# A four-layer graph network on one core: where the adjacency is checked for low bits, and where the branch on it stands

## The chip, the core and the metric

The kernel runs on one core of one Trainium2 chip. A core has TensorE (PE, matrix products into PSUM banks), VectorE (DVE), ScalarE (ACT), GpSimd (POOL) and SyncE (SP), which here issues most of the loads; each engine runs its own instructions in the order in which they were written for it, and waits on semaphores for the others. Transfers from main memory are done by DMA engines. The metric is the time of the program on the device, in microseconds (us).

## The reference

There are N = 2708 nodes with 128 features and an adjacency matrix of 2708 x 2708 in fp32. Four layers, each with a layer norm and a rectifier before it and a residual sum after it, use the adjacency:

```python
# layer 0: attention weights, used with adj.T twice
C = alpha_src[None, :] + alpha_dst[:, None]
Tau = adj_matrix.T * jnp.exp(jnp.maximum(0.2 * C, C))
att_weights = Tau / jnp.sum(Tau, axis=1, keepdims=True)
Z = adj_matrix.T * att_weights @ H
# layer 1: relu of (normalised adj + identity) @ x @ weight
# layer 2: adj.T @ x / degree, two linear maps, batch norm, relu
# layer 3
Z1 = leaky_relu(s_row[:, None] + s_col[None, :], negative_slope=0.01)
den = jnp.exp(Z1)
num = jnp.matmul(A, den)
att = jnp.where(num != 0, den / jnp.where(num != 0, num, 1.0), 0.0)
H = jnp.matmul(A, jnp.matmul(att, XW))
```

In the inputs the adjacency holds only zeros and ones.

## The kernel before

The adjacency and its transpose lie in main memory. It is worked through in T = 22 tiles of 128 rows (the last has 20), each 2708 wide; a width is also split in six blocks of up to 512 columns (one PSUM bank each), or in two halves of 1536 and 1172 columns (COLS).

Layer 0 is in lines 274 to 420. A first loop (298 to 313) over the six blocks makes the layer norm, its transposes, the rows `row_a` of exponentials and the projections `hs`. A second loop (347 on) goes over the 22 tiles. For each half of a tile, ScalarE makes `tau` (L355), VectorE finishes it and multiplies it by the adjacency (L358, L361), and TensorE adds up `hs` times the result into six accumulators (`aggregate`, L224) and the column sums (L367). ScalarE also sums the degrees of each tile (`degrees`, L341). The tiles come through a pool `stream` of NSTREAM = 4 buffers, so a load waits until all readers of an older tile are done. For the last two tiles the aggregation is kept back, and the degree is summed on VectorE (L339). The accumulators are then copied to `hT` (`evacuate`, L215 and L217).

Layers 1 to 3 use a cheaper form of fp32 products where a matrix can be taken to be exact in a shorter format. TensorE multiplies tiles of type fp32r ("float32r"): the adjacency is converted to it (by ScalarE and VectorE, `rows`), and the other operand is split in a high and a low part. This is right only if no entry of the adjacency has bits set in the low half of its 32. So `check` (L292 to L294) reads the lower 16 bits of each element of a tile on ScalarE and writes their sum into a column of `low`. It runs once per tile in layer 0: for the first three tiles in the first loop (L310), for the others with the degrees (L345). Its other output, as wide as the tile, is thrown away into a buffer `junk`.

After layer 0 these sums become one number, `flag` (L395 to L402). All engines read it and branch (L1289, L1290):

```python
some_low = nc.values_load(flag[0:1, 0:1], min_val=0, max_val=1, skip_runtime_bounds_check_because="0 or 1")
with tc.If(some_low > 0) as general:
    with ExitStack() as s3:
        rest(False, s3)
with general.Else():
    with ExitStack() as s3:
        rest(True, s3)
```

`rest(exact, stack3)`, from L486, is layers 1 to 3. With these inputs the second side, with exact = True, is executed. Layers 1 and 2 (`product_by_halves`, L248) stream the matrix in halves of tiles, through dflat (three places, filled ahead at L388 during layer 0), row_b and pools; each half is converted (L529) and multiplied (L224). Layer 1 starts with `finish0` (L555), which turns the accumulators of layer 0 back, adds the residual and makes the layer norm, with `dis`, made from the degrees, as a factor.

Layer 3 sorts the nodes, takes sums of rows, and then has 22 steps (L1183 on): products into two PSUM banks in turn (L1206), a logarithm on ScalarE that frees each bank (L1211), a subtraction on VectorE (L1214), an exponential on ScalarE (L1220) and the product into the accumulators (L1150). These are copied out (L1235), turned and split (L1241, L1242). Last comes `product` (L232, called in L1287), over all 22 tiles of the transposed adjacency: `load_rows` (L1271) brings a tile into one of six places in turn, ScalarE (tiles 0 to 3) or VectorE (the others) converts it (L1283), TensorE multiplies it by the two parts. The last four tiles (NLAST) are done block by block, and `finish3` (L1247) copies each block, turns it, adds the residual and stores it.

The order of instructions on an engine comes from a scheduler that may move them by priority, except where `tc.keep_in_program_order` holds them; it does so within one side of a branch and not across it.

Of the kernel before, what the change touches and what calls it, by code (L numbers as in the profile page):

```python
# [8 lines left out]
F32 = mybir.dt.float32  # L9
# [10 lines left out]
def kernel(  # L20
# [19 lines left out]
    nc = tc.nc  # L40
# [46 lines left out]
    const = ctx.enter_context(tc.tile_pool(name="const", bufs=1))  # L87
# [13 lines left out]
    nc.vector.memset(xs[:, TF:, :], 0.0)  # L101
    for t0 in range(0, TF, 4):
        t1 = min(t0 + 4, TF)
        nc.sync.dma_start(
            xs[:, t0:t1, :], x[t0 * P : t1 * P, :].rearrange("(t p) d -> p t d", p=P)
        )
    nc.sync.dma_start(xs[:TAIL, TF, :], x[TF * P :, :])
# [166 lines left out]
    with ExitStack() as stack:  # L274
        stream = stack.enter_context(tc.tile_pool(name="stream", bufs=NSTREAM))
        edge = stack.enter_context(tc.tile_pool(name="edge", bufs=3))

        def load_rows(src, t):
            return fill(stream.tile([P, N], F32, tag="a", name="a"), src, t)

        low = const.tile([P, T], F32, name="low")
        nc.gpsimd.memset(low, 0.0)

        def junk(t):
            return dflat[:, :N] if t < 8 else hT[:, :N]  # L290

        def check(t, a):  # L292
            lower = a.bitcast(U16).rearrange("p (n h) -> p n h", h=2)[:, :, 0]
            return nc.scalar.activation(junk(t), lower, AF.Identity, accum_out=low[:, t : t + 1])  # L294

        first_rows = []
        done = 0
        for b in range(NB):
            layernorm(b, hn)
            p = bank()  # L300
            turned(p, hn, TILES[b])
            nc.vector.tensor_copy(hT[:, spans(b)], p[:, : len(TILES[b]) * P])
            p = acc_bank(b % 2)
            w = len(TILES[b]) * P
            nc.tensor.matmul(p[:, :w], w0_spread[:, 1, :], hT[:, spans(b)], start=True, stop=True)
            tc.keep_in_program_order(nc.scalar.activation(row_a[:, spans(b)], p[:, :w], AF.Exp, scale=-0.8))
            if b < 3:
                first_rows.append(load_rows(adj, b))
            else:
                tc.keep_in_program_order(check(b - 3, first_rows[b - 3]))  # L310
            while done < T and min(done + 3, T) <= TILES[b][-1] + 1:
                project(w0_ext, done, acc_bank(2 + done // 3 % 2))
                done += 3
        e_hi = const.tile([P, T], F32, name="e_hi")
        e_lo = const.tile([P, T], F32, name="e_lo")
        e_neg = const.tile([P, T], F32, name="e_neg")
        nc.scalar.activation(e_hi, hs[:, :, P], AF.Exp)
        nc.scalar.activation(e_lo, hs[:, :, P], AF.Exp, scale=0.2)
        nc.vector.tensor_scalar_mul(e_neg, e_hi, -1.0)
        pick = const.tile([P, NB, NB], F32, name="pick")  # L320
        nc.vector.memset(pick, 0.0)
        for b in range(NB):
            nc.vector.memset(pick[:, b, b : b + 1], 1.0)


        GR = 3
        ones_at = const.tile([P, NB // GR, 32], F32, name="ones_at")
        nc.vector.memset(ones_at, 0.0)
        for i in range(NB // GR):
            nc.vector.memset(ones_at[:, i, i : i + 1], 1.0)  # L330
        deg = const.tile([P, T], F32, name="deg")
        nc.gpsimd.memset(deg, 0.0)
        accs = [acc_bank(b) for b in range(NB)]
        den = bank()
        waiting = []

        def degrees(t, a):
            if t >= T - 2:
                nc.vector.tensor_reduce(deg[:, t : t + 1], a, AX.X, ALU.add)  # L339
            else:  # L340
                m = nc.scalar.activation(junk(t), a, AF.Identity, accum_out=deg[:, t : t + 1])  # L341
                if t < 3:
                    tc.keep_in_program_order(m)
            if t >= 3:
                check(t, a)  # L345

        for t in range(T):
            a = first_rows[t] if t < 3 else load_rows(adj, t)
            late = t >= T - 2
            rhs = (yT, row_b)[t % 2]  # L350
            for h, (h0, h1) in enumerate(COLS):
                w = h1 - h0
                tau = edge.tile([P, w], F32, tag=f"tau{h}", name=f"tau{h}", bufs=3)
                at2 = rhs[:, h0:h1]
                nc.scalar.activation(  # L355
                    tau[:, :w], row_a[:, h0:h1], AF.Relu, bias=e_neg[:, t : t + 1], scale=e_lo[:, t : t + 1]
                )
                nc.vector.scalar_tensor_tensor(  # L358
                    tau[:, :w], tau[:, :w], e_hi[:, t : t + 1], a[:, h0:h1], ALU.add, ALU.mult
                )  # L360
                nc.vector.tensor_mul(at2[:, :w], a[:, h0:h1], tau[:, :w])  # L361
                if not late:
                    aggregate(hs[:, t, :P], rhs, accs, t == 0, False, range(3 * h, 3 * h + 3))
                for b in range(3 * h, 3 * h + 3):
                    lo, hi = E0[b]
                    g = 32 * (b % GR)
                    nc.tensor.matmul(  # L367
                        den[g : g + 32, : hi - lo],
                        ones_at[:, b // GR, :],
                        tau[:, lo - h0 : hi - h0],  # L370
                        start=(t == 0 and b < GR),
                        stop=(t == T - 1 and b >= GR),
                    )
            waiting.append((t, a))
            if t >= 2:
                degrees(*waiting.pop(0))
            if t == 6:
                w1_sb = load("w1_sb", [P, P], w1, nc.sync)
                wn_sb = load("wn_sb", [P, P], w_n, nc.sync)
                wc_sb = load("wc_sb", [P, P], w_c, nc.sync)  # L380
                w3_sb = load("w3_sb", [P, P], w3, nc.sync)
            if t == 8:
                a3s = vectors("a3s", (a3[0, :P], a3[0, P:]), nc.sync)
                vecs = vectors("vecs", (b_n, b_c, gamma, beta), nc.sync)
            if t == T - 4:

                for i in range(3):
                    fill_half(dflat[:, i * CUT : (i + 1) * CUT], adj_t, i, 0)  # L388
            if t == 10:
                wn_t = transposed("wn_t", wn_sb)  # L390
                wc_t = transposed("wc_t", wc_sb)
                w3_ext, _ = with_scores("w3_ext", w3_sb, transposed("w3_t", w3_sb), a3s)
        for t, a in waiting:
            degrees(t, a)
        low_all = const.tile([P, 1], F32, name="low_all")  # L395
        nc.vector.tensor_reduce(low_all, low, AX.X, ALU.add)
        p = bank()
        nc.tensor.matmul(p[:1, :1], low_all, ones[:, 0:1], start=True, stop=True)
        flag_f = const.tile([1, 1], F32, name="flag_f")
        nc.vector.tensor_scalar(flag_f, p[:1, :1], 0.0, None, ALU.is_gt)  # L400
        flag = const.tile([1, 1], I32, name="flag")
        nc.vector.tensor_copy(flag, flag_f)  # L402
        deg1 = const.tile([P, T], F32, name="deg1")
        nc.vector.tensor_scalar_add(deg1, deg, 1.0)
        dis = const.tile([P, T], F32, name="dis")
        inv_sqrt(dis, deg1, 1e-8)
        den_sb = small.tile([32 * GR, 512], F32, tag="den_sb", name="den_sb", bufs=1)
        nc.vector.tensor_copy(den_sb, den[: 32 * GR, :])
        dent = bank()
        for q in range(4):  # L410
            nc.tensor.transpose(dent[:, q * 96 : (q + 1) * 96], den_sb[:, cols(q)], ident[:96, :96])
        rden = const.tile([P, 4, GR, NB // GR], F32, name="rden")
        nc.vector.reciprocal(rden, dent[:, : 4 * 96].rearrange("p (q g r) -> p q g r", g=GR, r=32)[:, :, :, : NB // GR])
        for b in range(NB):
            for t in (T - 2, T - 1):
                aggregate(hs[:, t, :P], (yT, row_b)[t % 2], accs, False, t == T - 1, [b])
            evacuate(b, hT, accs[b])
        rdeg = const.tile([P, T], F32, name="rdeg")
        nc.vector.scalar_tensor_tensor(rdeg, deg, 0.0, deg, ALU.is_equal, ALU.add)
        nc.vector.reciprocal(rdeg, rdeg)  # L420
# [869 lines left out]
    with tc.If(some_low > 0) as general:  # L1290
        with ExitStack() as s3:
            rest(False, s3)
# [35 lines left out]
```

## Time and profile before

| What | us |
|---|---|
| median of 3 runs | 850.79 (850.65 to 852.95) |
| the profiled execution | 853.49 |
| its span, first to last instruction | 851.7 |
| busy: TensorE / VectorE / ScalarE / GpSimd | 729.7 / 583.7 / 536.1 / 189.2 |

The mean granted clock of TensorE is 0.932. In the span, layer 0 lasts until about 204, layers 1 and 2 until about 400, layer 3's tables until about 530, its 22 steps until about 778, and the last product until the end. A line of the timeline gives start, duration, engine, line of the kernel, operation, what it writes and reads, and how many were merged; in brackets it gives the idle time before it and who ended that. TensorE's ends are modelled, so its starts are better evidence than its busy time. "issue" is a wait for which the profile shows no cause.

### The profile page before, as it was taken

The page shows a single profiled execution, that of the slowest core. Times are in us where ns is not written, and L with a number is a line of the kernel's source. Part 1 is how long each engine was busy: PE and PEld are TensorE (multiplying, and loading weights), DVE is VectorE, ACT ScalarE, POOL GpSimd, SP SyncE. Part 2 cuts the span into 40 slices and gives each one's busy share as a digit, 9 for nine tenths or more (in the row PEclk, how much of TensorE's full clock was granted, in tenths as well). Part 3 has the DMA queues.
Part 4 walks back from the last instruction along what each step waited for, and adds up shares of the span by engine and source line. Part 5 has one row for each costly group of instructions (what it writes and reads, how often), then busy time and mean ns, then how long its engine had stood idle before and what let it go on. Part 6 is the DMA issues. An engine that isn't in the chain of part 4 may idle for free.

```text
span 851.7 us, 9005 instructions
## 1 busy us (share of the span) xinstructions
PE 729.7 (86%) x3113; PEld 440.8 (52%) x3113; DVE 583.7 (69%) x1112; ACT 536.1 (63%) x595; POOL 189.2 (22%) x161
## 2 busy tenths in 40 slices
PE   3599999995996979978649785798999989989997
PEld 2333333332775858756216531555555555555785
DVE  5499879786824363447988967776666666655854
ACT  3889999995845473437860026678778777767000
POOL 3000000012201010002000113446666666620010
PEclk9899999997897989988879995899999999999999
DMA  9044444723997989975505985677777776785994
GB/s 339 3 148 180 177 164 182 305 78 148 355 393 284 365 330 395 419 294 208 186 0 184 401 333 210 239 282 272 273 257 287 263 279 255 278 306 229 404 427 139
DMA packets 39476, 218.63 MB, mean 257 GB/s; under 512 B 5108, under 2 KB 13999, under 8 KB 25359
## 3 DMA queue, kind: packets, MB, share of 16 engines
q1 hardware_dynamic: 27704, 150.19, 45.6%
q0 software_dynamic: 8624, 65.76, 21.1%
q10 hardware_dynamic: 3090, 1.99, 0.7%
q8 instruction: 27, 0.44, 0.2%
q14 instruction: 31, 0.25, 0.1%
HBM read 214.12 MB, written 3.79 MB: 256 GB/s over the span
## 4 chain that ended last, share of the span: by engine, by line
PE 14%; DMA 12%; DVE 9%; issue 6%; POOL 6%; ACT 5%; SPq 0%; DVEq 0%; POOLq 0%; ACTq 0%
PE acc L1150 4%; PE bank L1206 4%; DMA hs<-in_adj_t_dram 4%; DMA row_b<-pre_d,pre_i 3%; PE acc L835 2%; DMA row_b<-in_adj_t_dram 2%; ACT rows L1168 2%; POOL hT L647 2%; POOL hs L647 1%; DMA yT<-pre_d,pre_i 1%; PE acc L224 1%; POOL row_b L647 1%; ACT row_a L747 1%; DVE rows L1283 1%; DVE bits L744 1%
## 5 line engine op out<-in xcount | busy, mean ns | idle before, releaser
L1206 PE MATMUL bank<-rows,d_hi 128*128 128x512 f32 (+1 forms) x264 | 106.5, 408 | 24.4 <-ACT ln L1211 12.7
L224 PE MATMUL acc<-rows,h_hi 128*128 128x512 f32 (+1 forms) x264 | 106.5, 408 | 10.3 <-ACT rows L529 6.0
L1150 PE MATMUL acc<-e,xw 128*128 128x512 f32 (+1 forms) x264 | 104.3, 545 | 0.0
L1211 ACT ACTIVATE ln<-bank,tiny 128x512 f32<-128x512 f32 x132 | 79.8, 632 | 33.1 <-PE bank L1206 32.9
L1206 PE MATMUL bank<-rows,d_lo 128*128 128x512 f32 (+1 forms) x264 | 98.7, 385 | 0.0
L224 PE MATMUL acc<-rows,h_lo 128*128 128x512 f32 (+1 forms) x264 | 98.0, 388 | 0.2 <-DVE h_lo L506 0.2
L1214 DVE TENSOR_TENSOR e<-e,ln 128x1536 f32<-128x1536 f32 (+2 forms) x66 | 70.0, 1097 | 15.9 <-ACT ln L1211 15.6
L1206 PEld LDWEIGHTS bank<-rows,d_hi 128*128 128x128 f32 x264 | 51.6, 195 | 53.1 <-ACT ln L1211 31.7
L358 DVE SCALAR_TENSOR_TENSOR tau<-tau,e_hi,a 128x1536 f32<-128x1536 f32 (+1 forms) x44 | 70.5, 1623 | 9.7 <-DMA a<-in_adj_dram 5.6
L1150 PEld LDWEIGHTS acc<-e,xw 128*128 128x128 f32 x264 | 48.4, 190 | 52.6 <-issue 52.6
L355 ACT ACTIVATE tau<-row_a,e_neg,e_lo 128x1536 f32<-128x1536 f32 (+1 forms) x44 | 65.7, 1504 | 3.3 <-PE bank L367 3.2
L224 PEld LDWEIGHTS acc<-rows,h_hi 128*128 128x128 f32 x264 | 52.5, 199 | 24.3 <-ACT rows L529 8.3
L367 PE MATMUL bank<-tau,ones_at 128*32 128x512 f32 (+1 forms) x264 | 51.8, 566 | 8.3 <-DVE tau L358 8.3
L224 PEld LDWEIGHTS acc<-rows,h_lo 128*128 128x128 f32 x264 | 52.6, 200 | 11.8 <-issue 1.9
L1220 ACT ACTIVATE e<-e 128x2708 f32<-128x2708 f32 x22 | 54.1, 2461 | 3.3 <-DVE e L1214 3.3
L224 PE MATMUL acc<-yT,hs 128*128 128x512 f32 x132 | 56.1, 563 | 0.0
L224 PE MATMUL acc<-row_b,hs 128*128 128x512 f32 x132 | 55.3, 557 | 0.0
L1206 PEld LDWEIGHTS bank<-rows,d_lo 128*128 128x128 f32 x264 | 51.6, 195 | 7.0
L224 PE MATMUL acc<-rows,y_hi 128*128 128x512 f32 x132 | 49.8, 384 | 3.8 <-DVE rows L1283 1.9
L224 PE MATMUL acc<-rows,y_lo 128*128 128x512 f32 x132 | 48.4, 382 | 0.0
L529 ACT CAST rows<-dflat 128x1536 fp32r<-128x1536 f32 (+1 forms) x26 | 34.2, 1330 | 20.6 <-DMA dflat<-in_adj_dram 11.2
L1189 DVE TENSOR_SCALAR xw<-xw,c_exp 128x128 f32<-128x128 f32 x22 | 6.4, 290 | 58.2 <-DMA xw<-xw_d,xw_i 58.2
(411 smaller groups left out, 1415.4 us busy)
## 6 DMA issues: line engine op xcount, KB each, us to landing
a<-in_adj_dram SPq DMA_DIRECT2D x21, 1354.0 KB
rows<-in_adj_t_dram SPq DMA_DIRECT2D x16, 1354.0 KB
dflat<-in_adj_t_dram SPq DMA_DIRECT2D x9, 768.0 KB
rows<-in_adj_t_dram SPq DMA_DIRECT2D x9, 768.0 KB
dflat<-in_adj_dram SPq DMA_DIRECT2D x9, 768.0 KB
rows<-in_adj_dram SPq DMA_DIRECT2D x9, 768.0 KB
dflat<-in_adj_t_dram SPq DMA_DIRECT2D x5, 1354.0 KB
hs<-in_adj_t_dram SPq DMA_DIRECT2D x5, 1354.0 KB
```

The source lines that it names most:

```text
L224: nc.tensor.matmul(accs[b][:, : hi - lo], w, moving[:, lo - at : hi - at], start=start and i == 0, stop=stop and i == len(parts) - 1,)
L355: nc.scalar.activation(tau[:, :w], row_a[:, h0:h1], AF.Relu, bias=e_neg[:, t : t + 1], scale=e_lo[:, t : t + 1])
L358: nc.vector.scalar_tensor_tensor(tau[:, :w], tau[:, :w], e_hi[:, t : t + 1], a[:, h0:h1], ALU.add, ALU.mult)
L367: nc.tensor.matmul(den[g : g + 32, : hi - lo], ones_at[:, b // GR, :], tau[:, lo - h0 : hi - h0], start=(t == 0 and b < GR), stop=(t == T ...
L529: m = nc.vector.tensor_copy(r, a) if i % 2 and i > 4 else nc.scalar.copy(r, a)
L647: return nc.gpsimd.indirect_dma_start(out=out, out_offset=None, in_=src, in_offset=bass.IndirectOffsetOnAxis(ap=idx, axis=0),)
L835: m = nc.tensor.matmul(accs[b][64 * h : 64 * h + 2 * NC, : hi - lo], w[:r, t, :], a[:r, lo:hi], start=(t == 0 and i == 0), stop=(t == T - ...
L1150: m = nc.tensor.matmul(accs[b][:, : hi - lo], xw, e[:, lo:hi], start=(s == 0), stop=(s == NE - 1))
L1206: m = nc.tensor.matmul(num[:, : hi - lo], d, a[:, lo:hi], start=(i == 0), stop=(i == len(products) - 1))
L1211: nc.scalar.activation(ln[:, lo:hi], num[:, : hi - lo], AF.Ln, bias=tiny)
L1214: tc.keep_in_program_order(nc.vector.tensor_sub(e[:, beg:hi], e[:, beg:hi], ln[:, beg:hi]))
L1220: tc.keep_in_program_order(nc.scalar.activation(e, e, AF.Exp))
```

## The change

The check leaves layer 0. It is made in the last product, on the tile as loaded, on ScalarE, beside the conversion; its thrown-away output goes to `row_a`, which nothing reads any more there. Layers 1 to 3 follow layer 0 without a branch, with exact = True. After them come the flag and one branch: if some low bit was found, the nodes are loaded again, layer 0 is done again, and layers 1 to 3 with exact = False, and the outputs are written anew. Layer 0 and the load of the nodes become functions (`layer0`, `load_nodes`) so that they can be placed twice, and `const` keeps its tiles by name, so that the second pass uses the same ones. With these inputs the second pass is jumped over.

```diff
-    nc.vector.memset(xs[:, TF:, :], 0.0)
...
+    def load_nodes():
+        nc.vector.memset(xs[:, TF:, :], 0.0)
...
+    load_nodes()
...
-        low = const.tile([P, T], F32, name="low")
-        nc.gpsimd.memset(low, 0.0)
...
-        def check(t, a):
-            lower = a.bitcast(U16).rearrange("p (n h) -> p n h", h=2)[:, :, 0]
-            return nc.scalar.activation(junk(t), lower, AF.Identity, accum_out=low[:, t : t + 1])
...
-            if b < 3:
-                first_rows.append(load_rows(adj, b))
-            else:
-                tc.keep_in_program_order(check(b - 3, first_rows[b - 3]))
...
+                if b < 3:
+                    first_rows.append(load_rows(adj, b))
...
-            if t >= 3:
-                check(t, a)
...
-        low_all = const.tile([P, 1], F32, name="low_all")
-        nc.vector.tensor_reduce(low_all, low, AX.X, ALU.add)
-        p = bank()
-        nc.tensor.matmul(p[:1, :1], low_all, ones[:, 0:1], start=True, stop=True)
-        flag_f = const.tile([1, 1], F32, name="flag_f")
-        nc.vector.tensor_scalar(flag_f, p[:1, :1], 0.0, None, ALU.is_gt)
-        flag = const.tile([1, 1], I32, name="flag")
-        nc.vector.tensor_copy(flag, flag_f)
...
+    layer0()
...
                 r = steps.tile([P, N], F32R, tag="rows", name="rows")
                 m = nc.scalar.copy(r, a) if t < 4 else nc.vector.tensor_copy(r, a)
                 tc.keep_in_program_order(m)
+                lower = a.bitcast(U16).rearrange("p (n h) -> p n h", h=2)[:, :, 0]
+                nc.scalar.activation(row_a[:, :N], lower, AF.Identity, accum_out=low[:, t : t + 1])
                 return r
...
+    low = const.tile([P, T], F32, name="low")
+    nc.gpsimd.memset(low, 0.0)
+    with ExitStack() as s3:
+        rest(True, s3)
+    low_all = const.tile([P, 1], F32, name="low_all")
+    nc.vector.tensor_reduce(low_all, low, AX.X, ALU.add)
+    p = bank()
+    nc.tensor.matmul(p[:1, :1], low_all, ones[:, 0:1], start=True, stop=True)
+    flag_f = const.tile([1, 1], F32, name="flag_f")
+    nc.vector.tensor_scalar(flag_f, p[:1, :1], 0.0, None, ALU.is_gt)
+    flag = const.tile([1, 1], I32, name="flag")
+    nc.vector.tensor_copy(flag, flag_f)
     some_low = nc.values_load(flag[0:1, 0:1], min_val=0, max_val=1, skip_runtime_bounds_check_because="0 or 1")
-    with tc.If(some_low > 0) as general:
+    with tc.If(some_low > 0):
+        load_nodes()
+        layer0()
         with ExitStack() as s3:
             rest(False, s3)
-    with general.Else():
-        with ExitStack() as s3:
-            rest(True, s3)
```

## The prediction

> **What bounds the kernel now.** I read the busy time by stretches first, to find the stages; then the groups of the layer-0 loop by shape; then the timeline of each engine at the four places that the change touches: the start of the loop, its pace, the branch, and the last product.
>
> Busy time by stretches (us; per engine busy and count in the order PE, weight loads, DVE, ACT, POOL; then granted clock, DMA share, GB/s):
>
> ```profile
> 43.00:200.00 157.00, 156.82 (x535) 57.09 (x533) 140.41 (x105) 153.66 (x122) 4.29 (x2) 0.99 0.45 167
> ...
> 778.00:852.00 74.00, 64.50 (x312) 52.32 (x310) 46.37 (x74) 11.75 (x8) 2.36 (x1) 0.97 0.80 322
> ```
>
> In the layer-0 loop (43 to 200) ScalarE is busy 153.7 of 157 us and TensorE looks full too. In the last product (778 to 852) ScalarE has 11.75 us of work and DMA moves 322 GB/s. So the check leaves a stage where ScalarE is full for one where it is nearly idle. The groups of the loop, by shape:
>
> ```profile
> L294 ACT ACTIVATE hT<-a 128x2708 f32<-128x2708 uint16 x14 | 34.3, 2450 | 0.1
> ...
> L355 ACT ACTIVATE tau<-row_a,e_neg,e_lo 128x1536 f32<-128x1536 f32 x20 | 33.1, 1656 | 0.0
> ...
> L341 ACT ACTIVATE hT<-a 128x2708 f32<-128x2708 f32 x12 | 29.3, 2446 | 0.0
> L355 ACT ACTIVATE tau<-row_a,e_neg,e_lo 128x1172 f32<-128x1172 f32 x21 | 28.4, 1352 | 3.2 <-PE bank L367 3.2
> ```
>
> One step of the loop costs ScalarE two scores (L355), one degree sum (L341) and one low-bit check (L294). In the timeline these start 1.56, 1.26, 2.44 and 2.44 us apart, 7.70 us a step. TensorE shows which engine sets the pace, by the starts of the aggregation:
>
> ```profile
> 71.48 2.84 PE L224 MATMUL acc<-yT,hs 128*128 128x512 f32 x6
> ...
> 78.39 2.84 PE L224 MATMUL acc<-row_b,hs 128*128 128x512 f32 x6
> ...
> 164.55 2.84 PE L224 MATMUL acc<-row_b,hs 128*128 128x512 f32 x6
> ...
> 172.30 2.84 PE L224 MATMUL acc<-yT,hs 128*128 128x512 f32 x6
> ```
>
> Early steps are 6.91 us apart (78.39 − 71.48), TensorE's own pace, as it had a store of finished tiles; late ones 7.75 (172.30 − 164.55), ScalarE's pace. The change of pace comes after t = 14 (start 141.28). At the start of the loop three checks stand ahead of the exponentials that the loop needs:
>
> ```profile
> 28.72 2.45 ACT L294 ACTIVATE dflat<-a 128x2708 f32<-128x2708 uint16 x1
> ...
> 36.79 0.25 ACT L317 ACTIVATE e_hi<-hs 128x22 f32<-128x22 f32 x1
> ```
>
> At the branch:
>
> ```profile
> 200.08 0.08 DVE L402 CAST flag<-flag_f 1x1 int32<-1x1 f32 x1
> ...
> 203.88 1.28 ACT L1179 ACT_TABLE_LOAD   x1 [3.47 <-issue]
> ...
> 205.08 1.94 PE L198 MATMUL bank<-ident,hT 128*128 128x128 f32 x8 [5.26 <-DVE bias L603]
> ...
> 212.22 1.46 ACT L529 CAST rows<-dflat 128x1536 fp32r<-128x1536 f32 x1
> ...
> 213.71 6.23 SPq L77 DMA_DIRECT2D dflat<-in_adj_t_dram  x3
> ```
>
> The flag is there at 200.16; the next instruction of any engine starts at 203.88; the transposes of layer 1 start at 205.08; the first converted tile, on which the first product waits, ends at 213.68, and SyncE goes on loading at 213.71. From 216 to 300 DMA is busy about 0.9 of the time, so layers 1 and 2 start when loading starts. The end of the attention and the last product, ScalarE and then VectorE:
>
> ```profile
> 771.30 2.46 ACT L1220 ACTIVATE e<-e 128x2708 f32<-128x2708 f32 x1 [1.24 <-DVE e L1214]
> ...
> 778.98 2.45 ACT L1283 CAST rows<-hT 128x2708 fp32r<-128x2708 f32 x1
> ```
>
> ```profile
> 794.45 1.57 DVE L1283 CAST rows<-dflat 128x2708 fp32r<-128x2708 f32 x1
> ...
> 836.33 1.57 DVE L1283 CAST rows<-hs 128x2708 fp32r<-128x2708 f32 x1 [2.52 <-DMA hs<-in_adj_t_dram]
> ```
>
> VectorE's conversion at 836.33 had waited for its rows, as all from 812.69 on did, 3.25 us apart: the last product is bound by its loads from 796 on.
>
> **What the Trainium skill says.** "ScalarE: Activation LUTs", section "What ACT_TABLE_LOAD costs", gives an ACTIVATE with immediate operands 186 ns + 0.833 ns an element: an estimate of 2.44 us for 2708; the trace has 2.45, on 16-bit halves (L294) as on fp32 (L341). "Runtime: NRT & Kernel Launch", section "Instruction fetch mechanics", says that a taken branch to a far target stalls for a fetch of its instructions; the trace agrees with 3.7 us from flag to next instruction. "TensorE: Matmul & The Clock Gate", Part 1, says that an idle TensorE falls to half clock; the windows show 0.50 from 204 to 216, after the gap. It stays so after the change, since the gap there shrinks but does not vanish.
>
> **The change part by part** (all in times of the profiled execution, span 851.7).
>
> *Start of the loop.* Three checks leave 28.72 to 36.79. The last input of the exponentials, the projection copy on VectorE, ends at 33.16, so they start at 33.2 in place of 36.79: −3.6. That is less than the 3 × 2.7 removed, as VectorE and TensorE hold the rest.
>
> *Pace.* ScalarE's step falls to 7.70 − 2.44 = 5.26 us, VectorE's is 6.04, TensorE's 6.91: TensorE sets it. Of 22 checks only five steps (15 to 19) had been late, (180.06 − 141.28) − 5 × 6.91 = 4.2: −4.2. Together t = 19 starts at 172.2, not 180.06.
>
> *End of the loop.* From 172.2: its step up to the last sums 6.9 (179.1), the sums for t = 20 and 21 at 1.97 each (183.0), 24 aggregations of the two last tiles at 0.43 (4 of them 0.13) 9.1, four transposes 0.5: 192.6, where before it was 199.8. Beside it VectorE multiplies t = 21 until 179.5, sums two degrees (2 × 2.95), and POOL's power (3.85) gives the scaling by 190.4: hidden.
>
> *Branch gone.* Layer 1's transposes follow at 192.7 and not 205.08. From the first use of them (206.21) to the first product (213.73) it takes 7.5: so 193.7 + 7.5 = 201.2 against 213.73: **−12.5**. Loading: the five loads that started at 203.90 wait now for the last readers of row_b and of the old row buffers, 189 to 193, so 11 to 15 earlier; the two agree. The instructions of layers 1 to 3 come in the same order on every engine until the last attention step, so I carry 12.5 through unchanged. A table load (1.28 at 203.88) goes too, hidden.
>
> *Checks in the last product.* In the built order five of the 22 checks stand among the last attention step: after the second, fourth and sixth logarithm, after the last exponential, and before the third copy. The logarithms free the two PSUM banks that TensorE refills, so these count. Laid out in times of before: check 0 from 766.8, logarithms 3 and 4 by 770.5, check 1 to 772.9, logarithms to 773.9, check 2 to 776.4, exponential 776.4 (before 771.30): +5.1. Then the products of the last step end at 783.5 (778.5), and check 4 puts the third copy to 784.9 and the first conversion to 785.4 (before 778.98): +6.4. The rows for checks 0 to 3 were issued between 747.5 and 763.0 and a load lands in some 7 us, so I cost no wait for them.
>
> Behind the conversions stand the loads: SyncE loads row 6 when the first conversion has ended, 787.8 (781.46 before). Before, DMA ran dry, since row 10 waited for VectorE (conversion at 794.45) until 796.04; now loads 6 to 20 run on without a hole: 787.8 + 4.4 + 15 × 3.25 = 841.0, against 836.2. (The 4.4 is from before: 836.2 − 796.04 − 11 × 3.25.) So **+4.8**: the loads win some of the 6.4 back. The 17 remaining checks at 2.63 (their spacing back to back, 193.62 to 196.25) are faster than the loads at 3.25, so ScalarE catches up at about row 13. After the last big row two checks precede the first copy: 5.2 us, against 5.1 from 836.21 to 841.31: +0.1.
>
> *Flag and branch at the end.* The sum over the flags lies before VectorE's copies and is hidden there; the two tiny flag operations after its last addition (847.08) cost 0.4. The branch takes 3.7 as at 200.16. Beside it the last output lands at about 850.0 and the end follows 1.7 later. From SyncE's last issue, 848.33 + 3.7 = 852.0, against 850.0: **+2.0**. Its bounds: 0.5, if the load of the flag overlaps, and 3.5, if fetch and closing barrier come one after the other.
>
> Sum: −12.5 + 4.8 + 0.1 + 2.0 = −5.6. The profiled execution took 853.49 (span 851.7 and 1.8 around it), 2.7 above the median of 850.79; I take the difference from the median: **845.2 us**. Bounds: start −10 to −14.5 (the clock gate and loading), last product +3 to +8.5 (the order above, or a check that waits for its row), end +0.5 to +3.5.
>
> **Rivals.**
> A. Full relief passes and the tail is cheap: start −14.5, tail +3, end +0.5: −11, 839.8. For it: the loads idle from 183 to 204 now; against: the order puts checks before the exponential.
> B. The gains are spent: TensorE is the true bound of layer 0, loading in layers 1 and 2 absorbs half of what is left, and the checks cost all 6.4: −8 + 6.5 + 2 = +0.5, 851.3, no difference. For it: TensorE at 156.8 of 157; against: 7.75 against 6.91 a step.
> C. Slower: ScalarE becomes the bound of the last product. From the fourth conversion's end (794.8) it has 17 checks; at 2.63 us they keep up with the loads and end at 846.1, and from (846.1 − 794.8) / 17 = 3.0 us each they set the end. At 3.8, if conversions and loads in the same memory slow them, the end moves by 17 × 3.8 − 51.3 = 13.3: 845.2 + 13.3 = 858.5; slower than before from 3.5 us on. For it: 16-bit halves are read at every second place, beside a VectorE that converts; against: the same read takes 2.44 to 2.63 in layer 0, with VectorE busy too.
> D. The change does not do what it says: no; in the built order the branch stands behind the outputs, and no check is left in layer 0.
>
> **How the numbers follow.** My case 0.70 (842 to 848.5), A 0.12, B 0.10, C 0.08. The range 840 to 850.5 leaves out some of A and nearly all of C. About 0.3% (2.6 us) is what a measurement can tell from no change: faster takes most of my case and A, 0.80; the same B and the edge of mine, 0.12; slower 0.08.
>
> **What would show it.** Right: the loop's steps 6.91 apart to the end; the first product of layer 1 near 201; the last exponential of the attention about 7.4 earlier than 771.30 (−12.5 + 5.1); the last rows about 7.7 earlier than 836.2; two to three us more after the last output. Wrong: steps above 7.2, a hole in loading at the start of layer 1, checks in the last product that start after their rows by more than 3 us, or a closing branch above 4 us.

## The result, and the profile after

The changed kernel took 859.18 us (median of 20 runs, 853.54 to 862.64), the kernel before it 852.36 us beside it (20 runs): a ratio of 1.0073, 95% interval 1.0054 to 1.0092. It is slower by some 6.2 us. The profiled execution after took 862.64 us (span 860.8), 3.5 above its median; the one before, 853.49 (span 851.7).

The front of the program did as forecast. ScalarE's timeline of the changed kernel, at the start of the loop and at the turn to layer 1 (start and duration in us):

```profile
32.01 0.24 ACT L327 ACTIVATE e_hi<-hs 128x22 f32<-128x22 f32 x1 [0.64 <-DVE hs L226]
...
199.45 1.46 ACT L530 CAST rows<-dflat 128x1536 fp32r<-128x1536 f32 x1
```

TensorE's timeline, its late steps and the first product of layer 1:

```profile
165.99 2.84 PE L240 MATMUL acc<-yT,hs 128*128 128x512 f32 x6
...
172.90 2.84 PE L240 MATMUL acc<-row_b,hs 128*128 128x512 f32 x6
...
200.96 1.22 PE L240 MATMUL acc<-rows,h_hi 128*128 128x512 f32 x2 [0.77 <-ACT rows L530]
```

The loop starts at 32.0 in place of 36.8, its late steps are 6.91 apart (172.90 − 165.99) and no longer 7.75, and layer 1's first product stands at 200.96, where it stood at 213.73: 12.8 us won.

At the other end, the last attention step and the start of the last product on ScalarE:

```profile
753.44 2.45 ACT L1287 ACTIVATE row_a<-hT 128x2708 f32<-128x2708 uint16 x1
...
757.02 2.47 ACT L1287 ACTIVATE row_a<-row_b 128x2708 f32<-128x2708 uint16 x1
...
760.30 2.48 ACT L1287 ACTIVATE row_a<-hs 128x2708 f32<-128x2708 uint16 x1
...
762.75 2.48 ACT L1221 ACTIVATE e<-e 128x2708 f32<-128x2708 f32 x1
765.10 2.47 ACT L1287 ACTIVATE row_a<-yT 128x2708 f32<-128x2708 uint16 x1
...
770.33 2.47 ACT L1287 ACTIVATE row_a<-dflat 128x2708 f32<-128x2708 uint16 x1
...
773.25 2.46 ACT L1284 CAST rows<-hT 128x2708 fp32r<-128x2708 f32 x1
```

These are the five checks that the prediction spoke of, in the places where it put them. And SyncE's last issue of an output, before the change and after it:

```profile
847.97 0.36 SPq L1263 DMA_DIRECT2D out_dram<-xs  x1
```

```profile
843.19 0.61 SPq L1264 DMA_DIRECT2D out_dram<-xs  x1
```

That issue ended at 848.33 before and ends at 843.80 now. So the work itself is over 4.5 us earlier than before, of the 12.8 won. What makes the kernel slower than before comes behind it. From there to the end of the span, which is called the closing from here on, it was 3.4 us (848.33 to 851.7) and is 17.0 (843.80 to 860.8). The windows show that no engine computes in that time; after the bounds and the length come busy times in the order PE, weight loads, DVE, ACT, POOL:

```profile
844.00:861.00 17.00, 0.00 (x0) 0.00 (x0) 0.00 (x0) 0.00 (x0) 0.00 (x0) 0.50 0.06 17
```

What fills it are instructions that don't count as busy. They stand under the line of the branch (L1308) and under the line that closes the program (L1340). The columns are queue, operation and count, the shortest, median and longest duration in ns, and the first and last start in us. The branch:

```profile
L1308 ACTq COMPARE_BRANCH  x1: 50/50/50, 843.8 to 843.8; - x1
L1308 PEldq COMPARE_BRANCH  x1: 3542/3542/3542, 843.9 to 843.9; - x1
...
L1308 ACTq EVENT_SEMAPHORE  x1: 17/17/17, 847.0 to 847.0; - x1
...
L1308 POOLq INC_SWDGE_SEM  x1: 2440/2440/2440, 848.3 to 848.3; - x1
```

The closing line, after the change:

```profile
L1340 POOLq DRAIN  x3: 46/107/9215, 850.8 to 860.6; - x3
```

and the closing line of the kernel before:

```profile
L1323 POOLq DRAIN  x3: 46/108/11626, 820.8 to 851.4; - x3
```

After the flag, TensorE's queue takes 3.5 us over the branch. The other four are through it in 45 to 72 ns by their records, but stand still behind it too: ScalarE, which branched at 843.8, starts its next instruction at 847.0, before TensorE is through (847.4), and the last of them does at 848.1. At 848.3 GpSimd has an INC_SWDGE_SEM, an instruction on a semaphore, which takes 2.4 us, and at 850.8 it begins a drain of 9.2 us, to 860.0; short semaphore instructions and drains of all engines follow, 0.8 us. Before the change the same drain was there, and cost nothing: it began at 820.8, together with GpSimd's last memset (2.36 us, so 11.63 − 2.36 = 9.27 for the drain), beside the last product. GpSimd had nothing left to do then, so its queue ran ahead to the end of the program. With a branch at the end, it must wait there for the flag.

### The profile page after: what moved, and what is told of

Its sections match the earlier page's. It is cut to its first block, busy times and chain, and to the rows that moved or that the text cites. A ratio compares the mean times of both kernels' runs of the same rounds, so it can differ in the third digit from the quotient of the medians.

```text
span 860.8 us, 9041 instructions
## 1 busy us (share of the span) xinstructions
PE 728.1 (85%) x3113; PEld 439.9 (51%) x3113; DVE 582.8 (68%) x1112; ACT 538.1 (63%) x594; POOL 189.7 (22%) x161
## 4 chain that ended last, share of the span: by engine, by line
PE 38%; DVE 16%; DMA 14%; POOL 12%; issue 9%; ACT 9%; SPq 0%; POOLq 0%; DVEq 0%; ACTq 0%
PE acc L240 22%; PE bank L374 5%; DMA hs<-in_adj_t_dram 4%; POOL hs L648 3%; POOL hT L648 2%; POOL row_b L648 2%; DMA row_b<-in_adj_t_dram 2%; DMA rows<-in_adj_t_dram 2%; POOL rstd L189 2%; PE bank L1207 2%; POOL yT L648 2%; PE acc L1151 2%; DMA yT<-pre_d,pre_i 1%; POOL xw L648 1%; DMA row_b<-pre_d,pre_i 1%
## 5 line engine op out<-in xcount | busy, mean ns | idle before, releaser
L1151 PE MATMUL acc<-e,xw 128*128 128x512 f32 (+1 forms) x264 | 106.2, 552 | 2.5 <-ACT e L1221 2.5
L374 PE MATMUL bank<-tau,ones_at 128*32 128x512 f32 (+1 forms) x264 | 49.3, 567 | 4.7 <-DVE tau L365 4.7
```

The lines of the kernel that those rows point to most:

```text
L374: nc.tensor.matmul(den[g : g + 32, : hi - lo], ones_at[:, b // GR, :], tau[:, lo - h0 : hi - h0], start=(t == 0 and b < GR), stop=(t == T ...
L1151: m = nc.tensor.matmul(accs[b][:, : hi - lo], xw, e[:, lo:hi], start=(s == 0), stop=(s == NE - 1))
```

## The experiments

Theory 1: the closing costs it, by the drain that now starts behind the flag. Rival 1: the checks in the last product cost it. Rival 2: the long drain belongs to the branch or to what it skips, so that it can't be had earlier. The ratios below are to the kernel before, run beside each.

**Without the branch.**

```diff
-    some_low = nc.values_load(flag[0:1, 0:1], ...)
-    with tc.If(some_low > 0):
-        load_nodes()
-        layer0()
-        with ExitStack() as s3:
-            rest(False, s3)
```

> The changed kernel without its last part: the load of the flag, the branch on it and the second pass in fp32 are left out; the checks and the sum over their flags stay. Theory 1 (the closing costs it: GpSimd has to pass the branch, so its drain of 9.2 us starts only behind the flag): GpSimd's drain starts right behind its last memset, near 818, as before the change; the last output is issued near 843.2 and the span ends 3.4 later, near 847; 4 to 5 us faster than before, ratio about 0.995. Rival 1 (the checks in the last product cost it): nothing is won, time as after the change, ratio about 1.007.

Measured: 841.61 us, 0.9889 (0.9858 to 0.9921). The closing line:

```profile
L1334 POOLq DRAIN  x3: 46/102/11632, 807.5 to 839.0; - x3
```

GpSimd's drain starts at 807.5 with the memset, and from the last output's issue (836.63) to the end of the span (839.3) it is 2.7 us. Rival 1 falls as the whole cause: with all checks in place the kernel is faster than before. It is so by 5 us more than expected, as its work ended at 836.6 and not at 843.8. 3.5 of that is the changed kernel's profiled execution, which lay so far above its own median; the rest is within the interval.

**An early drain.** One instruction, behind GpSimd's last memset and ahead of the load of the flag:

```diff
+    tc.keep_in_program_order(nc.gpsimd.drain())
     low_all = const.tile([P, 1], F32, name="low_all")
```

> The changed kernel with one drain more on GpSimd, behind its last memset and ahead of the load of the flag. Theory 1: this drain takes about 9.2 us near 818, beside the last product; the one behind the branch falls to about 0.1 us, so the closing falls from 17.0 to about 7.8 us (branch 3.5, semaphores, 2.4 for INC_SWDGE_SEM, barrier 0.8); span near 851.6, ratio to before about 0.999. Rival 2 (the long drain belongs to the branch, or to INC_SWDGE_SEM just ahead of it, and not to what GpSimd had done before): the closing drain stays at 9.2 us, closing 17, ratio about 1.007.

Measured: 847.87 us, 0.9955 (0.9934 to 0.9976): from slower to faster than before by this line alone. The new drain, then branch and closing:

```profile
L1299 POOLq DRAIN  x1: 11617/11617/11617, 811.6 to 811.6; - x1
```

```profile
L1341 POOLq DRAIN  x3: 34/47/107, 844.1 to 845.5; - x3
```

It takes the 9.26 us (less the memset) at 814, hidden, and the longest drain behind the branch is 107 ns. The closing is 6.5 us (839.29 to 845.8) and not 7.8, since INC_SWDGE_SEM fell too, from 2440 to 189 ns. Rival 2 falls.

**A late GpSimd in the kernel before.** No branch is near the end there; one tiny copy that reads the last result:

```diff
         with ExitStack() as s3:
             rest(True, s3)
+            seen = const.tile([P, 1], F32, name="seen")
+            nc.gpsimd.tensor_copy(seen[:TAIL, :], xs[:TAIL, TF, 0:1])
```

> The kernel before the change, with one tiny copy on GpSimd that reads the last result (20 x 1 elements) added at the very end. Theory 1: this alone moves GpSimd's drain from 823 to about 847.3, where it takes 9.2 us with no branch near it: the end goes from 851.7 to about 857.5, +6, ratio about 1.007. Rival 2 (the branch makes the drain long): the drain is short and nothing changes, ratio 1.000.

Measured: 856.47 us, 1.0070 (1.0042 to 1.0098). A copy of 0.18 us costs 6 us, as it holds back what stands behind it:

```profile
L1325 POOLq DRAIN  x3: 46/108/9446, 843.2 to 853.2; - x3
```

9.45 less the copy is 9.27 again, some 90 us after the last gather was issued. In the kernel before it was 9.27 some 72 us after the last gather, in the changed one 9.22 some 112 us after it. So it isn't a wait for transfers to land; what it does in that time no run shows.

**Without the checks.**

```diff
-                lower = a.bitcast(U16).rearrange("p (n h) -> p n h", h=2)[:, :, 0]
-                nc.scalar.activation(row_a[:, :N], lower, AF.Identity, accum_out=low[:, t : t + 1])
```

> The changed kernel without the 22 low-bit checks in the last product (that part of the computation is left out, so the flag is always 0); flag, branch and second pass stay. Theory 1: the attention's last exponential starts about 4 to 5 us earlier than 762.75 and the last output is issued about 5 to 8 us earlier than 843.2, near 836 to 838; the closing stays 17 us: span about 853 to 855, ratio about 1.000 to 1.003, still not faster than before. Rival 1: most of the loss goes with the checks, and the time falls to that of before less the 12.8 won ahead of layer 1, ratio about 0.985.

Measured: 850.75 us, 0.9974 (0.9959 to 0.9990), closing 17.2 us (834.35 to 851.5). The checks cost 8.4 us ((1.0073 − 0.9974) × 852), not 4.9; and with all of them gone the kernel is still only 0.26% faster than the one before, though its work ends 14 us earlier. That is neither of the two forecasts: the checks cost more than theory 1 gave them, and the closing, with them gone, still keeps the kernel from a ratio of 0.985.

**Without the first five checks only.**

```diff
+                if t < 5:
+                    return r
                 lower = a.bitcast(U16).rearrange("p (n h) -> p n h", h=2)[:, :, 0]
```

> The changed kernel without the checks of tiles 0 to 4 (that part of the computation is left out); the 17 others, flag, branch and second pass stay, closing 17 us. Prediction's account (only the five checks that stand in the last attention step and ahead of the third copy put off the loads): as with all checks left out, ratio about 0.997 to 0.999. Rival (each check holds its tile's buffer for 2.5 us more, so the later 17 put off the loads): close to the changed kernel, about 1.005 to 1.007.

Measured: 850.62 us, 0.9972 (0.9954 to 0.9990), the same as without all 22. So the five in the last attention step and ahead of the third copy cost all of it, and the 17 others nothing that these intervals (1.5 us each way) could show: in the changed kernel they start 2.6 us apart at first, and from 800.12 to 813.07 they follow the rows, 3.24 us apart.

**A near branch.** The second pass replaced by one memset:

```diff
     with tc.If(some_low > 0):
-        load_nodes()
-        layer0()
-        with ExitStack() as s3:
-            rest(False, s3)
+        nc.vector.memset(xs[:, TF:, :], 0.0)
```

> The changed kernel with the second pass in fp32 replaced by one small memset of VectorE (that part of the computation is left out), so that the branch jumps over next to nothing; checks, flag and branch stay. If the branch's 3.5 us on TensorE's queue are the fetch of a far target: COMPARE_BRANCH there falls to about 0.1 us, no INC_SWDGE_SEM is left, but the drain of 9.2 us still starts behind the flag: closing about 17.0 - 3.5 - 2.4 = 11 us, 6 us faster than the changed kernel, ratio about 1.000. If any taken branch costs it: closing 13 to 14.5, ratio 1.003 to 1.005. If the drain goes with the second pass (it belongs to the skipped gathers): closing 5 us or less, ratio 0.993.

Measured: 850.45 us, 0.9974 (0.9950 to 0.9999). The branch, then the closing:

```profile
L1308 PEldq COMPARE_BRANCH  x1: 223/223/223, 839.8 to 839.8; - x1
```

```profile
L1337 POOLq DRAIN  x3: 46/107/9215, 840.0 to 849.8; - x3
...
L1337 ACTq DRAIN  x2: 8/8/8, 839.9 to 849.5; - x2
```

TensorE's branch falls from 3542 to 223 ns, ScalarE goes on 0.1 us after its own (839.7) where it stood still for 3.1, no INC_SWDGE_SEM is left, and the drain is the same 9.2: closing 10.4 us (839.74 to 850.1). Of the 6.6 us less, 2.4 are INC_SWDGE_SEM and 4.2 the branch on all engines. So the branch's price goes with what it jumps over (its length and its content changed together here), which agrees with the Trainium skill, "Runtime: NRT & Kernel Launch", section "Instruction fetch mechanics"; and the drain has nothing to do with what is skipped, as it is the same with nearly nothing to skip. By the ratios this kernel gains 8.4 us on the changed one, where its closing is 6.6 shorter; the rest is within the two intervals.

**What sets the drain.** A drain in the middle of the attention besides the early one; in the first run:

```diff
                 if s >= 3:
                     fetch_xw(s)
+                if s == 6 and not exact:
+                    tc.keep_in_program_order(nc.gpsimd.drain())
```

> The changed kernel with two more drains on GpSimd: one at the start of attention step 6, when about 39 of its 110 gathers have been issued, one behind its last memset. What sets the 9.2 us: if the number of gathers issued since the last drain, the first drain takes about 3.3 and the second about 5.9 us; if it is a fixed price once gathers have been issued, both take 9.2; if the first drain has to see transfers land as well, it takes 9.2 and more and the second 9.2. In each case the drain behind the branch takes 0.1 us.

The pass that runs is the one with `exact` true, so this drain stood in the second pass and never ran. The run only repeats the early drain (842.40 us, one run; 11.63 us for the drain with its memset). With `if s == 6 and exact:`

> The early drain, and one drain more at the start of attention step 6 of the pass that runs, when 40 of GpSimd's 112 transfers have been issued. If the 9.2 us go with the number issued since the last drain: 3.3 us for the first, 5.9 for the second (plus the 2.36 of the memset ahead of it). If they are a fixed price: 9.2 for each. If a drain has to see transfers land: the first, with gathers just issued, takes longer than its share. The drain behind the branch 0.1 us in each case.

Measured, one run: 849.12 us. The first drain, and the two gathers (indexed transfers) that GpSimd still issued while the drain stood in its queue (GpSimd's timeline):

```profile
L1188 POOLq DRAIN  x1: 7153/7153/7153, 579.8 to 579.8; - x1
```

```profile
580.04 2.30 POOL L648 DMA_INDIRECT hs<-pre_d,pre_i  x1 [2.54 <-DMA hs<-in_adj_t_dram,row_i]
582.64 0.96 POOL L648 DMA_INDIRECT xw<-xw_d,xw_i  x1 [0.30 <-issue]
```

and the second:

```profile
L1301 POOLq DRAIN  x1: 8337/8337/8337, 813.9 to 813.9; - x1
```

From the last gather's end (583.60) the first drain took 3.35 us (579.8 + 7.15 = 586.95), after 40 transfers; the second, less the memset, 5.98, after 72 more. Together 9.33, and 84 and 83 ns a transfer, as 9.27 us are 83 ns for each of 112: in this one execution the price goes with the transfers that GpSimd issued since its last drain.

**The early drain, with five checks moved.** The first five checks are taken from the last product as well. Layer 1 reads the same rows of the transposed adjacency as halves, so the checks went there (`checked`: tiles 0 to 4), with five columns more in `low`:

```diff
                 m = nc.vector.tensor_copy(r, a) if i % 2 and i > 4 else nc.scalar.copy(r, a)
                 tc.keep_in_program_order(m)
+                if t < checked:
+                    lower = a.bitcast(U16).rearrange("p (n h) -> p n h", h=2)[:, :, 0]
+                    c = t if h == 0 else T + t
+                    nc.scalar.activation(row_a[:, :w], lower, AF.Identity, accum_out=low[:, c : c + 1])
                 return r
```

> The changed kernel with the early drain on GpSimd, and with the checks of tiles 0 to 4 moved from the last attention step and the start of the last product to the two sweeps of layer 1, where the same tiles of the transposed adjacency pass as halves (10 checks of 1.47 or 1.16 us on ScalarE, which is busy 52 of 90 us there). If the first five checks are what the last product loses by (8.4 us, the difference of the runs with and without all checks) and ScalarE has the room in layer 1: 8 us faster than with the early drain alone, ratio to before about 0.986. If the 17 other checks cost it, or layer 1's loads wait for the checks: ratio 0.993 to 0.996 as with the early drain alone.

Measured: 848.58 us, 0.9944 (0.9924 to 0.9963), nothing beyond the early drain. The 8 us were won at the end and lost in layers 1 and 2, from ScalarE's first to its last conversion 163.4 us (198.0 to 361.4) where the early drain alone has 153.3. ScalarE's timeline at the turn between the halves of layer 1, with the checks (L535):

```profile
240.84 1.19 ACT L535 ACTIVATE row_a<-rows 128x1172 f32<-128x1172 uint16 x1
...
244.18 1.20 ACT L535 ACTIVATE row_a<-dflat 128x1172 f32<-128x1172 uint16 x1
...
260.58 1.12 ACT L582 ACTIVATE o<-bank,dis 128x128 f32<-128x128 f32 x4
```

and with the early drain alone:

```profile
250.81 2.15 ACT L578 ACTIVATE o<-bank,dis 128x128 f32<-128x128 f32 x8
```

The last ReLUs of the first half end at 261.7 and not at 253.0: the checks stand among them, and the last four now come behind a layer norm for which ScalarE waited 3.9 us. So the next version takes tiles 15 to 19, whose checks fall elsewhere, and lets the last product begin with these. The checks of the second halves also write their thrown-away output to a part of row_b here; before, a load into row_a on GpSimd had waited 5.5 us for them, but the instruction behind that load wasn't late by it (it waited 2.9 us more for VectorE).

```diff
+    EARLY_T = [15, 16, 17, 18, 19]
...
+        order = [*EARLY_T, *[t for t in range(T) if t not in EARLY_T]]
...
-            product(list(range(T)), y_of, load_rows, range(NB), finish3)
+            product(order, y_of, load_rows, range(NB), finish3)
```

> The early drain, and five checks moved to layer 1 again, but of tiles 15 to 19, where ScalarE waits 1 to 3.6 us for each of its rows; the last product takes these five tiles first. If the move of tiles 0 to 4 lost its gain because its checks of the second half fell on the turn between the halves of layer 1 (240 to 253), where ScalarE's evacuations and ReLUs queued behind them: layers 1 and 2 take 153 us again from first to last conversion in place of 163, and the time falls by 8 us from that with the early drain alone, to a ratio of about 0.986. If any check in layer 1 holds up its loads: 0.993 to 0.996 as before.

Measured: 847.55 us, 0.9947 (0.9930 to 0.9963). Layers 1 and 2 were back at 154.9 us, as expected, and still nothing was won: from the first conversion of the last product to the last output's issue it was 73.3 us (763.48 to 836.76), with the early drain alone 69.5 (769.24 to 838.69). TensorE's timeline shows the new wait:

```profile
774.03 1.62 PE L240 MATMUL acc<-rows,y_hi 128*128 128x512 f32 x3 [1.05 <-DVE y_hi L1249]
```

With the early drain alone:

```profile
771.75 0.50 PE L240 MATMUL acc<-rows,y_hi 128*128 128x512 f32 x1 [3.11 <-ACT rows L1284]
```

The first product waits for y of tile 15, 10.6 us behind the first conversion, where it waited only for the conversion, 2.5 behind it. The last version is `EARLY_T = [10, 11, 12, 13, 14]`:

> As the run with tiles 15 to 19, but with tiles 10 to 14, whose columns of y are scaled earlier. If that run lost its last 3.7 us because the last product began with tile 15, whose y comes behind the evacuation of the fourth block (from its first conversion to its last output 73.3 us, in place of 69.5): this falls back to 69.5, and the ratio goes from 0.9947 to 0.990. If the order of the tiles is not what costs it: 0.994 to 0.995 again.

Measured: 845.09 us, 0.9923 (0.9895 to 0.9952). The last product took 70.3 us (765.86 to 836.19), nearly as expected, but layers 1 and 2 took 156.5, so that 3 us of the 8 went there. It is faster than the kernel before and than the changed one. Whether it beats the early drain alone is not shown, as their intervals overlap. What these three runs say of where the time went rests on one profiled execution each.

## Why the prediction was wrong

The forecast was −5.6 us. In the terms of its own sum, against the two profiled executions (862.64 − 853.49 = +9.1):

| term | forecast | measured |
|---|---|---|
| layer 1's first product | −12.5 | −12.8 (213.73 to 200.96) |
| checks in the last product | +4.9 | +8.3 (work ends −4.5 in place of −12.8); 8.4 and 8.6 by the times of the runs without them, 7.1 by the means below |
| flag and branch at the end | +2.0 | +13.6 (17.0 less 3.4) |

By the ratio of all runs the difference is less, 6.2 us, since the profiled execution after lay 3.5 above its median and the one before 1.1. The closing was 17.0 to 17.2 in all three kernels with the far branch and no early drain, so the scatter is in the work ahead of it.

**The step that failed is "Flag and branch at the end: +2.0", bounds 0.5 to 3.5.** It counted the branch (3.7 behind the last issue; TensorE was through it 3.6 behind, at 847.4) and set the landing of the last output beside it. It didn't ask what else each engine had to do in order to end. GpSimd's queue held a drain of 9.3 us that the profile of before showed under its closing line, from 820.8 on. It was never priced, because it cost nothing there: the cover was that GpSimd came to the end early. The branch took the cover away. Of the 13.6 us, the early drain gave back 10.5 (17.0 to 6.5: 9.2 of the drain, 2.3 of INC_SWDGE_SEM, less 0.9 for what the closing then waits on beside them); what is left, 3.1, is inside the bounds that were given. All rivals carried the same small end, so none of them held the mechanism. Rival C's 858.5 us lies near the 859.2 measured; that is luck, as its cause isn't there (below). Of the signs named for an error, "a closing branch above 4 us" comes nearest: the branch itself kept to some 4 us, what followed it did not.

**Start, pace and branch gone: right in mechanism and sum.** The first product of layer 1 stands at 200.96, forecast at 201.2. The parts were each off by one or two us and made up for it: the loop's first aggregation came 4.8 us earlier (39.68 for 44.46), forecast 3.6; the pace won 2.4 more up to t = 19 (172.90), forecast 4.2, as the late steps won their 4.2 but steps 8 to 11 took 29.8 us (94.76 to 124.52) where they had taken 28.3; the transposes started at 192.79, forecast 192.7. That the sum came out within 0.3 is partly luck. TensorE's half clock behind the gap stayed, as forecast, but more briefly: 0.50 from 200 to 204 and 1.00 from 208 on, where it had been 0.50 from 204 to 216.

**The checks in the last product: right in place and in the delay that they make; what failed is the gain set against it.** From the last exponential but one to the first conversion it was 18.0 us before (760.94 to 778.98) and is 24.6 (748.66 to 773.25). Over the six profiles with all checks it is 23.7 in the mean (22.0 to 25.5), over the four without the first five 17.7 (16.6 to 18.0): +6.1, forecast +6.4. Then the loads were to win 1.6 back, by running on without a hole. The hole is still there: row 10 waited for VectorE's first conversion (787.19 to 788.75) and was issued 6.0 us behind row 9, where it had been 7.5. Rows 6 to 10 were issued over 13.0 us in place of 14.6, but that is no gain of the change, since the kernel before with the late copy has 13.1 too. From the first conversion to the end of the last issue the same six profiles have 70.1 us in the mean (68.6 to 71.7) and the four 69.1 (68.8 to 69.4): +1.0 where −1.5 was forecast. So the term is about 7.1 us by the profiles, and not 4.9; the 8.4 from the times of the runs, with an interval of 2 each way, agrees.

**Rival C: its mechanism is not there.** The 17 checks behind the conversions take 2.47 us each, 2.6 apart where they stand back to back; the rival needed 3.0 and more. ScalarE has caught up with the rows by 796.80, and taking these checks away as well gained nothing.

## What to carry to other kernels

Where a change puts a wait or a branch at the end of a program, read each engine's queue behind its last busy instruction, not only its busy time: what an early engine does there is hidden only as long as it comes early. If GpSimd has issued many gathers, give it its drain where it is idle; here one line was worth 10 us. Work moved to "an idle engine" has to be placed by the stretch it falls in: ScalarE was busy 52 of 90 us in layer 1, and ten checks of 1.2 to 1.5 us there cost 10 us at the turn of the halves and 2 to 3 elsewhere.

## What the hardware showed that was not expected

- GpSimd's DRAIN took 3.35 us after 40 transfers issued by it, 5.98 after 72 and 9.27 after 112, and the last was the same 72 us after the last gather (kernel before), 94 us (late copy) and 112 us (changed kernel, 9.22). The Trainium skill, "VectorE: DVE Perf Modes", section "The DRAIN you can't avoid", tells two kinds of DRAIN apart: a flush behind each VectorE operation, and the runtime's own at the start and end of a program, about 12 ns on all five engines. GpSimd's drain here, at 83 ns for each of its transfers, is like neither. On the other queues the drains behind the branch took 7 to 17 ns; in the kernel before, those that began while outputs were still being made took up to 611 ns.
- INC_SWDGE_SEM behind the branch took 2440 ns with that drain still to come and 189 ns after it.
- TensorE's queue took 3542 ns over a taken branch past the whole second pass (3378 to 3702 in the other runs with it) and 223 past one memset. The other four took 45 to 72 ns in both by their records, but started their next instruction 3.1 to 4.0 us later behind the far branch and 0.1 to 0.4 behind the near one. Some of these may have waited for one another; at the branch of the kernel before, ScalarE and VectorE stood still for 3.47 us with a wait that the profile calls "issue". So the record of a branch doesn't hold all of its cost; the start of the next instruction shows it.
